# An LSTM with a mixture of experts behind it: when the router's small operations run, and which engine adds the residual

## The chip, the cores and the metric

One core of a Trainium2 chip runs the whole program. The metric is the device time of one execution in microseconds. The engines are PE (matrix products), DVE (VectorE), ACT (ScalarE), POOL (GpSimd) and SP, which starts transfers.

## The reference

Two sequences of 1,024 tokens with 256 features, all in float32. First an LSTM with 256 units over time, with a residual; then a layer of experts, with a residual again:

```python
def step(carry, xw_t):                     # 1024 times, one after the other
    prev_h, prev_c = carry
    a = xw_t + prev_h @ Wh                 # (2, 256) @ (256, 1024)
    i, f, o = sigmoid(a[:, :256]), sigmoid(a[:, 256:512]), sigmoid(a[:, 512:768])
    next_c = f * prev_c + i * tanh(a[:, 768:])
    next_h = o * tanh(next_c)
    return (next_h, next_c), next_h

x = x + lstm(x, h0=cond)                   # "x + h", called x2 in the kernel
shared = mean over 2 of  (silu(x @ w1.T) * (x @ w3.T)) @ w2.T     # hidden 512
s = sigmoid(concat(x, cond) @ W_router.T)  # 8 scores a token
# the two best of s + router_bias; gates = their s, divided by their sum
routed = sum over 8 of  gate[e] * (gelu(x @ r1[e].T) @ r2[e].T)   # hidden 256
out = x + (shared + routed) / 4
```

Only the LSTM is a chain: step t + 1 needs h of step t. The experts need x + h of their tokens and nothing else.

## The kernel before

**The recurrence.** A Python loop over `t` writes out 1,024 steps; `grp, u = divmod(t, 16)`. In each step PE multiplies h by the weights into two PSUM tiles (L541, 20 products, two records each in the profile), DVE transposes both (L568), ACT takes sigmoid and tanh (L571, L572), DVE and ACT make the new cell (L575, L579, L580, L588), and DVE the new h (L591, two halves). Each engine works through its instructions in the order in which the program issues them, so the order of issue decides what stands between two steps.

**Groups.** The tokens go through the experts in groups of steps, `GROUPS`: seven of 128 steps, then two of 64 (numbered 0 to 8; group 6 ends with step 895, group 7 with 959, group 8 with 1023). When a group's last step is done, `experts` puts its matrix products as units in a list `fill.pe`: 116 units for 128 steps, 90 for 64. They are worked off beside the steps of the following groups. `PACES` says in how many steps they should be done.

**The queues.** The class `Fill` holds a list for each engine. After the recurrent products of a step, `run_pe` issues up to two units (`ROOM`), or one where a projection of the inputs of the next 16 steps runs (u of 1, 6 or 11). Where fewer are issued, products with an identity matrix fill the place (L556). A unit that opens a PSUM bank is issued only if a bank is free; there are two (`fill.banks`), and `let_go` gives one back when DVE has read it. At the step's end, ACT's pieces are issued up to a cost of 1.0 (not where u is 8), and DVE's up to 0.5, first in first out; each piece carries a cost in the queue's own numbers and the first step in which it may run.

**DVE's pieces.** Of each shared product: multiply by the sigmoid (L340) and by the second product (L344); of each routed product: two multiplications (L364); then the sums: the start of a sum (L393) and one addition for each expert (L412, `add_expert`), which needs the gates of the router.

**The router.** PE makes the scores (L236), DVE adds the part of the condition (L254), ACT takes the sigmoid (L262), and `choose` lists 23 small DVE operations (L272 to L312) on 8 or 16 elements a partition, which end in the gates. `to_aside` puts them in the DVE queue with a cost of 0.18 each; only for the last group do they go to a list of their own, `aside`.

**x + h.** At the end of each 16th step (u of 15) `residual` adds x and the h of 16 steps on GpSimd into `x2T` (L485), and where a group ends it adds the one step left over. In the middle of the next 16 steps, DVE copies one element of it (`met`, L625), from u of 8 and t over 16 on.

**The end.** At step 1023 `drain` works off what is left of the groups before; then group 8 is put in, with six banks, and `drain` is called again: rounds of four units, ACT's pieces, DVE's pieces and three of `aside`. The outputs leave with a transfer for each 64 steps (L419).

Of the kernel before, what the change touches and what calls it, by code (L numbers as in the profile page):

```python
# [9 lines left out]
F32 = mybir.dt.float32  # L10
# [6 lines left out]
P = 128  # L17
# [6 lines left out]
TB = ROWS // N  # L24
# [11 lines left out]


ROOM = 2
WARM = 5
OUT_SCALE = 1.0 / (NS + TOP_K)  # L40
RSQRT2 = 0.7071067811865476
# [6 lines left out]
class Fill:  # L48
# [16 lines left out]
    def to_act(self, cost, fn, lag=0):  # L65
        self.add(self.act, cost, fn, lag)

    def to_dve(self, cost, fn, lag=1):
        self.add(self.dve, cost, fn, lag)

    def to_aside(self, cost, fn):
        if self.last:
            self.aside.append(fn)
        else:
            self.to_dve(cost, fn)

    def run_aside(self, count):
        for _ in range(min(count, len(self.aside))):
            self.aside.popleft()()

    def run(self, queue, budget):
        while queue and queue[0][0] <= self.step and queue[0][1] <= budget:
# [18 lines left out]
def lstm_moe_kernel(  # L101
# [16 lines left out]
    nc = tc.nc  # L118
# [57 lines left out]
    x2T = const.tile([P, K, T, N], F32, name="x2T")  # L176
# [4 lines left out]
    stepp = ctx.enter_context(tc.tile_pool(name="step", bufs=3))  # L181
# [4 lines left out]
    fill = Fill()  # L186

    def bank():
        if fill.last:
            pool, name = behind[0]  # L190
            behind.rotate(-1)
        else:
            pool, name = fill_ps, "ps_f"
        return pool.tile([P, 2, 256], F32, name=name)
# [10 lines left out]
    def condition_scores(lg, k):  # L205
        nc.tensor.matmul(
            lg, cond_b[:, k].rearrange("p s n -> p (s n)"), wr_sb[:, K + k, :],
            start=(k == 0), stop=(k == K - 1), skip_group_check=True,
        )
        if k == K - 1:  # L210
            fill.to_dve(0.25, lambda: keep_scores(lg))

    def keep_scores(lg):
        nc.vector.tensor_copy(cond_lg, lg)
        fill.let_go()

    def experts(t0, S):
# [10 lines left out]
        def toks(a, i):  # L228
            return a[:, i * P : (i + 1) * P]
# [13 lines left out]
        def big(name):  # L243
            return route.tile([P, NT, E], F32, name=name)
# [15 lines left out]
        def squash():  # L260
            st["s"] = big("s")
            nc.scalar.activation(st["s"], st["z"], AF.Sigmoid)  # L262
            for fn in choose():
                fill.to_aside(0.18, fn)

        def choose():

# [128 lines left out]
        def routed_down(i, e2, j):  # L396
            if j == 0:
                st["down"] = bank()
            ps, half, h = st["down"], j // (HR // P), j % (HR // P)
            c = (2 * e2 + half) * (HR // P) + h  # L400
            nc.tensor.matmul(  # L401
                ps[:, half, :], toks(st["h_r"][:, c, :], i), r2_sb[:, c, :],
                start=(h == 0), stop=(h == HR // P - 1), skip_group_check=True,
            )
            if j == 2 * (HR // P) - 1:
                for half in range(2):
                    fill.to_dve(0.5, lambda half=half: add_expert(i, 2 * e2 + half, ps[:, half, :]))

        def add_expert(i, e, ps):
            fill.run_aside(len(fill.aside))  # L410
            acc = st["acc", i]
            nc.vector.scalar_tensor_tensor(  # L412
                acc, ps, st["gate"][:, i, e : e + 1], acc, ALU.mult, ALU.add
            )
            if e % 2:
                fill.let_go()
            if e == E - 1:
                t = t0 + i * (P // N)
                nc.sync.dma_start(out=out_tn[t : t + P // N], in_=acc)  # L419
# [36 lines left out]
    def h_at(t):  # L456
        return hs[t // TB % 2][:, t % TB]

    def h_cols(t):
        u = t % TB  # L460
        return h_at(t)[:, :, N * u : N * (u + 1)]
# [16 lines left out]
    def gates_tile():  # L478

        tiles = [gates_ps.tile([P, 4, P], F32, name=f"ps{m}") for m in range(K)]  # L480
        return [a[:, 0] for a in tiles], [a[:, 1] for a in tiles], tiles[0][:, 2:]

    def residual(grp, u0, u1):
        t0 = grp * TB - 1
        nc.gpsimd.tensor_add(  # L485
            x2T[:, :, t0 + u0 : t0 + u1, :],
            xT_sb[:, :, t0 + u0 : t0 + u1, :],
            diags[grp % 2][:, u0:u1].rearrange("p u (k r) -> p k u r", r=ROWS)[:, :, :, :N],
        )

    ends, e0 = {}, 0
# [28 lines left out]
    nxt, nxt_turned, busy = gates_tile()  # L520
    for i in range(WARM):
        nc.tensor.matmul(
# [6 lines left out]
    for t in range(T):  # L529
        fill.step = t  # L530
        grp, u = divmod(t, TB)
        if u == 0:
            ps, turned = nxt, nxt_turned
            nxt, nxt_turned, busy = gates_tile()
            fresh = True
            sgm, gf = nxt_results


        for k, m, c0, c1 in BLOCKS:
            for q in range(Q):  # L540
                nc.tensor.matmul(  # L541
                    ps[m][q * ROWS : (q + 1) * ROWS][:, c0:c1],
                    h_at(t)[:, k, :],
                    wh_sb[:, k, q * D + m * P + c0 : q * D + m * P + c1],
                    start=False,
                    stop=(u == TB - 1 and k == K - 1),
                    skip_group_check=True,
                )
        ahead = t + TB < T and u in (1, 6, 11)
        if ahead:  # L550
            project(nxt, grp + 1, u // 5 - 1)
            fresh = False
        left = max(1, due - t)
        done = fill.run_pe(min(ROOM - ahead, -(-len(fill.pe) // left)))
        for _ in range(ROOM - done - ahead):
            nc.tensor.matmul(  # L556
                busy, ident, ident.unsqueeze(1).to_broadcast([P, 2, P]),
                start=fresh, stop=False, skip_group_check=True,
            )
            fresh = False  # L560
        rows = slice(N * u, N * (u + 1))

        gT = [turned[m].rearrange("p (a r) -> p a r", r=ROWS) for m in range(K)]
        c_new = [cells[m][:, t % 2] for m in range(K)]
        seen = [stepp.tile([P, N], F32, name=f"seen{m}") for m in range(K)]

        def transpose(m):
            nc.vector.transpose(turned[m], ps[m])  # L568

        def squash(m):  # L570
            nc.scalar.activation(sgm[:, u, m, :, :, 1], gT[m][:, 0:3, rows], AF.Sigmoid)  # L571
            nc.scalar.activation(gf[:, u, m, :, 0], gT[m][:, 3, rows], AF.Tanh)  # L572

        def forget(m):
            nc.vector.tensor_mul(gf[:, u, m, :, 1], sgm[:, u, m, 1, :, 1], c_prev[m][:, :, 1])  # L575

        def cell(m):

            nc.vector.tensor_copy(seen[m], gf[:, u, m, :, 0])  # L579
            nc.vector.tensor_tensor_scan(  # L580
                c_new[m].rearrange("p n z -> p (n z)"),
                sgm[:, u, m, 0].rearrange("p n z -> p (n z)"),
                gf[:, u, m].rearrange("p n z -> p (n z)"),
                0.0, ALU.mult, ALU.add,
            )

        def squash_cell(m):
            nc.scalar.activation(cells[m][:, 2, :, 0], c_new[m][:, :, 1], AF.Tanh)  # L588

        def output(m):  # L590
            nc.vector.tensor_mul(h_cols(t + 1)[:, m], sgm[:, u, m, 2, :, 1], cells[m][:, 2, :, 0])  # L591

        for fn in (transpose, squash):
            for m in range(K):
                fn(m)
        for m in range(K):
            forget(m)
            cell(m)
            squash_cell(m)
        for m in range(K):  # L600
            output(m)
        if u == TB // 2 and t + TB < T:
            nxt_results = results()
        else:
            fill.run(fill.act, 1.0)
        c_prev = c_new
        if u == TB - 1:
            residual(grp, int(grp == 0 or t - TB in ends), TB)
        if t == 2 * TB:
            lg = bank()[:, 0, :E]  # L610
            fill.banks -= 1
            fill.pe.extend((0, lambda k=k: condition_scores(lg, k)) for k in range(K))
        if t in ends:
            residual(grp + 1, 0, 1)
            if t == T - 1:
                drain(fill)
                fill.last = True
                fill.banks += 4
            t0, S, pace = ends[t]
            experts(t0, S)  # L620
            due = t + pace
        if u == TB // 2 and t > TB:

            met = stepp.tile([P, 1], F32, name="met")
            nc.vector.tensor_copy(met, x2T[:, 0, t - u - 2, :1])  # L625
        fill.run(fill.dve, 0.5)
    drain(fill)


def drain(fill):  # L630

    while fill.pe or fill.act or fill.dve:
        fill.step += 1
        fill.run_pe(4)
        fill.run(fill.act, 100.0)
        fill.run(fill.dve, 100.0)
        fill.run_aside(3)


# [63 lines left out]
```

## Time and profile before

| | |
|---|---|
| median of 3 runs | 2315.3 us (2314.7 to 2316.05) |
| profiled execution | 2314.89 us |
| its span, first to last instruction | 2313.1 us |
| granted clock of TensorE | 1.000 |
| busy: PE, DVE, ACT, POOL | 2220.1, 1701.6, 885.3, 25.9 us |
| L485 on POOL, 73 times | 328 ns median, 205 to 353 |
| L625 on DVE, 63 times | 9.2 us in all |

In a line of the profile's groups stand the line of the code, the engine, the operation, what is written from what is read, the shape of one instruction and the number of them; behind the bar the busy time in microseconds, the mean duration of one in nanoseconds, and the time that the engine stood idle just before them, with what ended it. A row of the timeline starts with the start and the duration in microseconds; PEld is the loading of weights, which may run ahead of the products. A row of the chain has start, duration and what was being done.

### The profile page before, as it was taken

How to read it: one execution, taken by the hardware profiler on the slowest of the kernel's cores; microseconds unless marked ns; L12 is line 12 of the kernel's file. 1: busy time of each engine (PE TensorE's matmuls, PEld its weight loads, DVE VectorE, ACT ScalarE, POOL GpSimd, SP SyncE). 2: the span in 40 equal slices, each digit the busy share in tenths (PEclk: the TensorE clock that was granted, in tenths of full speed). 3: DMA queues.
4: the chain of work that ended last, by engine and by line, in shares of the span. 5: the costliest groups of instructions: out<-in, count | busy, mean ns of one | idle time of the engine just before them, and what ended most of it. 6: DMA issues, size and time to landing. Idle time of an engine off the chain costs nothing.

```text
span 2313.1 us, 115407 instructions
## 1 busy us (share of the span) xinstructions
PE 2220.1 (96%) x48816; PEld 1574.3 (68%) x48816; DVE 1701.6 (74%) x10961; ACT 885.3 (38%) x6427; POOL 25.9 (1%) x82
## 2 busy tenths in 40 slices
PE   9999999999999999999999999999999999999978
PEld 6666666666666666666666666666666666666657
DVE  5666677777777777777777777777777777777775
ACT  3333334433334333443334333343333433344342
POOL 0000000000000000000000000000000000000000
PEclk9999999999999999999999999999999999999999
DMA  5000000000000000000000000000000000000000
GB/s 203 3 3 3 3 3 3 3 6 5 3 3 4 5 6 3 3 3 6 6 3 3 3 6 5 3 3 3 5 6 3 3 3 5 6 3 3 8 4 7
DMA packets 9705, 21.03 MB, mean 9 GB/s; under 512 B 1761, under 2 KB 7137, under 8 KB 8930
## 3 DMA queue, kind: packets, MB, share of 16 engines
q1 hardware_dynamic: 8898, 12.61, 1.6%
q8 instruction: 381, 6.24, 1.1%
q14 instruction: 138, 1.13, 0.2%
q10 hardware_dynamic: 288, 1.05, 0.1%
HBM read 11.56 MB, written 2.10 MB: 6 GB/s over the span
## 4 chain that ended last, share of the span: by engine, by line
DVE 59%; PE 37%; issue 3%; DMA 0%; SPq 0%; ACT 0%
PE ps L541 35%; DVE ps L568 29%; DVE c L580 12%; DVE results L575 8%; DVE seen L579 7%; DVE h L591 3%; PE ps L321 0%; PE ps_f L401 0%; PE ps_f L321 0%; PE ps L401 0%; DMA wh_sb<-in_wh_dram 0%; PE ps_f L383 0%; PE ps L383 0%; PE ps L556 0%; DVE acc L412 0%
## 5 line engine op out<-in xcount | busy, mean ns | idle before, releaser
L541 PE MATMUL ps<-wh_sb,h 128*32 128x128 f32 (+1 forms) x40960 | 1112.7, 254 | 86.9 <-DVE h L591 22.9
L541 PEld LDWEIGHTS ps<-wh_sb,h 128*32 128x32 f32 x40960 | 837.3, 109 | 489.9 <-DVE h L591 488.0
L568 DVE STREAM_TRANSPOSE ps<-ps 128x128 f32<-128x128 f32 x2048 | 677.8, 332 | 416.4 <-PE ps L541 415.0
L571 ACT ACTIVATE results<-ps 128x6 f32<-128x6 f32 x2048 | 362.9, 177 | 1167.3 <-DVE ps L568 1071.5
L556 PE MATMUL ps<-ident 128*128 128x256 f32 x1954 | 575.4, 391 | 0.0
L591 DVE TENSOR_TENSOR h<-results,c 128x2 f32<-128x2 f32 x2048 | 314.2, 153 | 168.2 <-ACT c L588 168.1
L556 PEld LDWEIGHTS ps<-ident 128*128 128x128 f32 x1954 | 351.4, 189 | 83.3 <-issue 45.1
L588 ACT ACTIVATE c<-c 128x2 f32<-128x2 f32 x2048 | 321.5, 157 | 220.1 <-DVE c L580 180.6
L580 DVE TENSOR_TENSOR_SCAN c<-results 128x4 f32<-128x4 f32 x2048 | 359.0, 175 | 0.0
L572 ACT ACTIVATE results<-ps 128x2 f32<-128x2 f32 x2048 | 340.4, 166 | 0.0
L579 DVE COPY seen<-results 128x2 f32<-128x2 f32 x2048 | 330.9, 162 | 0.0
L575 DVE TENSOR_TENSOR results<-results,c 128x2 f32<-128x2 f32 x2048 | 320.7, 157 | 0.0
L321 PE MATMUL ps_f<-x2T,r_sb 128*128 128x256 f32 (+1 forms) x800 | 166.8, 360 | 0.0
L321 PE MATMUL ps_f<-x2T,w_sb 128*128 128x256 f32 (+1 forms) x800 | 166.6, 360 | 0.0
L401 PE MATMUL ps_f<-r_sb,h_r 128*128 128x256 f32 x488 | 162.0, 424 | 0.0
L321 PEld LDWEIGHTS ps_f<-x2T,r_sb 128*128 128x128 f32 (+1 forms) x800 | 77.8, 153 | 42.7 <-issue 42.0
L321 PEld LDWEIGHTS ps_f<-x2T,w_sb 128*128 128x128 f32 (+1 forms) x800 | 77.6, 153 | 42.5 <-issue 41.8
L401 PEld LDWEIGHTS ps_f<-r_sb,h_r 128*128 128x128 f32 x488 | 75.4, 188 | 43.4 <-issue 40.5
L383 PE MATMUL ps_f<-w_sb,h_s 128*128 128x256 f32 x240 | 80.1, 425 | 0.0
L469 PE MATMUL ps<-wx_sb,xT_sb 128*32 128x128 f32 x2048 | 79.4, 273 | 0.0
L412 DVE SCALAR_TENSOR_TENSOR acc<-ps_f,gate,acc 128x256 f32<-128x256 f32 x122 | 58.2, 477 | 4.4 <-PE ps_f L401 4.2
L469 PEld LDWEIGHTS ps<-wx_sb,xT_sb 128*32 128x32 f32 x2048 | 58.6, 110 | 0.0
(81 smaller groups left out, 473.5 us busy)
## 6 DMA issues: line engine op xcount, KB each, us to landing
r_sb<-in_r_w1T_dram SPq DMA_DIRECT2D x1, 2048.0 KB, 17.2
r_sb<-in_r_w2T_dram SPq DMA_DIRECT2D x1, 2048.0 KB, 18.5
out_dram<-acc SPq DMA_DIRECT2D x16, 128.0 KB, 2.1
xT_sb<-in_xT_dram SPq DMA_DIRECT2D x6, 256.0 KB, 6.5
wx_sb<-in_wx_dram ACTq DMA_DIRECT2D x2, 512.0 KB, 4.2
wh_sb<-in_wh_dram SPq DMA_DIRECT2D x2, 512.0 KB, 4.4
w_sb<-in_s_w1T_dram SPq DMA_DIRECT2D x1, 1024.0 KB, 7.6
w_sb<-in_s_w3T_dram SPq DMA_DIRECT2D x1, 1024.0 KB, 9.6
```

The costliest lines, as they stand in the source:

```text
L321: nc.tensor.matmul(ps[r : r + rows, half, :W], w[:, k, c * P + r : c * P + r + rows], mov[k], start=(k == 0), stop=(k == K - 1), skip_grou ...
L401: nc.tensor.matmul(ps[:, half, :], toks(st["h_r"][:, c, :], i), r2_sb[:, c, :], start=(h == 0), stop=(h == HR // P - 1), skip_group_check= ...
L541: nc.tensor.matmul(ps[m][q * ROWS : (q + 1) * ROWS][:, c0:c1], h_at(t)[:, k, :], wh_sb[:, k, q * D + m * P + c0 : q * D + m * P + c1], sta ...
L556: nc.tensor.matmul(busy, ident, ident.unsqueeze(1).to_broadcast([P, 2, P]), start=fresh, stop=False, skip_group_check=True,)
L568: nc.vector.transpose(turned[m], ps[m])
L571: nc.scalar.activation(sgm[:, u, m, :, :, 1], gT[m][:, 0:3, rows], AF.Sigmoid)
L572: nc.scalar.activation(gf[:, u, m, :, 0], gT[m][:, 3, rows], AF.Tanh)
L575: nc.vector.tensor_mul(gf[:, u, m, :, 1], sgm[:, u, m, 1, :, 1], c_prev[m][:, :, 1])
L579: nc.vector.tensor_copy(seen[m], gf[:, u, m, :, 0])
L580: nc.vector.tensor_tensor_scan(c_new[m].rearrange("p n z -> p (n z)"), sgm[:, u, m, 0].rearrange("p n z -> p (n z)"), gf[:, u, m].rearrang ...
L588: nc.scalar.activation(cells[m][:, 2, :, 0], c_new[m][:, :, 1], AF.Tanh)
L591: nc.vector.tensor_mul(h_cols(t + 1)[:, m], sgm[:, u, m, 2, :, 1], cells[m][:, 2, :, 0])
```

## The change

The router's 23 operations always go to `aside`, and `run_dve` replaces the plain run of the DVE queue: it takes the head of the queue if that may run and fits into what is left of the budget, and otherwise one operation of `aside` for 0.18. An expert's addition is marked `late`: it doesn't run while `aside` holds anything. In steps with u of 15, DVE gets no piece; there it does `residual`, which moves from GpSimd to VectorE. The copy `met` goes. In `drain`, DVE's budget is 1.2 a round and covers both lists.

```diff
+ASIDE = 0.18
...
-    def to_dve(self, cost, fn, lag=1):
-        self.add(self.dve, cost, fn, lag)
-
-    def to_aside(self, cost, fn):
-        if self.last:
-            self.aside.append(fn)
-        else:
-            self.to_dve(cost, fn)
-
-    def run_aside(self, count):
-        for _ in range(min(count, len(self.aside))):
-            self.aside.popleft()()
+    def to_dve(self, cost, fn, lag=1, late=False):
+
+        self.dve.append((self.step + lag, cost, fn, late))
+
+    def run_dve(self, budget):
+        while True:
+            ready, cost, fn, late = self.dve[0] if self.dve else (0, 0.0, None, True)
+            if fn and ready <= self.step and cost <= budget and not (late and self.aside):
+                self.dve.popleft()
+            elif self.aside and budget >= ASIDE:
+                cost, fn = ASIDE, self.aside.popleft()
+            else:
+                return
+            budget -= cost
+            fn()
...
             nc.scalar.activation(st["s"], st["z"], AF.Sigmoid)
-            for fn in choose():
-                fill.to_aside(0.18, fn)
+            fill.aside.extend(choose())
...
-                    fill.to_dve(0.5, lambda half=half: add_expert(i, 2 * e2 + half, ps[:, half, :]))
+                    fill.to_dve(0.5, lambda half=half: add_expert(i, 2 * e2 + half, ps[:, half, :]), late=True)
 
         def add_expert(i, e, ps):
-            fill.run_aside(len(fill.aside))
...
     def residual(grp, u0, u1):
         t0 = grp * TB - 1
-        nc.gpsimd.tensor_add(
+        nc.vector.tensor_add(
...
         c_prev = c_new
-        if u == TB - 1:
-            residual(grp, int(grp == 0 or t - TB in ends), TB)
         if t == 2 * TB:
...
+        if u < TB - 1:
+            fill.run_dve(0.5)
+            continue
+        residual(grp, int(grp == 0 or t - TB in ends), TB)
         if t in ends:
             residual(grp + 1, 0, 1)
...
-        if u == TB // 2 and t > TB:
-
-            met = stepp.tile([P, 1], F32, name="met")
-            nc.vector.tensor_copy(met, x2T[:, 0, t - u - 2, :1])
-        fill.run(fill.dve, 0.5)
     drain(fill)
 
 
 def drain(fill):
 
-    while fill.pe or fill.act or fill.dve:
+    while fill.pe or fill.act or fill.dve or fill.aside:
         fill.step += 1
         fill.run_pe(4)
         fill.run(fill.act, 100.0)
-        fill.run(fill.dve, 100.0)
-        fill.run_aside(3)
+        fill.run_dve(1.2)
```

## The prediction

> **What bounds the kernel now.** I read the page first: busy shares, then the chain that ended last.
>
> ```profile
> PE 2220.1 (96%) x48816; PEld 1574.3 (68%) x48816; DVE 1701.6 (74%) x10961; ACT 885.3 (38%) x6427; POOL 25.9 (1%) x82
> ...
> DVE 59%; PE 37%; issue 3%; DMA 0%; SPq 0%; ACT 0%
> ...
> L568 DVE STREAM_TRANSPOSE ps<-ps 128x128 f32<-128x128 f32 x2048 | 677.8, 332 | 416.4 <-PE ps L541 415.0
> ...
> L556 PE MATMUL ps<-ident 128*128 128x256 f32 x1954 | 575.4, 391 | 0.0
> ```
>
> PE's 96% is padded: 1954 records (977 matmuls) of L556 only fill time. The chain is the LSTM recurrence: L541, transposes, cell, output, next step. DVE waits 415.0 us for L541, so there is a gap of about 0.4 us a step in which DVE's pieces run unseen. Taking the first L568 of each step from the timeline, 1,002 of 1,023 step intervals are 2.21 us, with no piece (512 steps) as with the costliest, L412 at 0.477 us together with L625 at 0.146 us (12 steps). The rest: three early steps (8, 11 and 15), and 18 steps of 2.29 us, all with u = 15. The timeline at one of these (step 447):
>
> ```profile
> 999.22 0.70 PE L321 MATMUL ps_f<-x2T,r_sb 128*128 128x256 f32 x2
> ...
> 1000.00 0.35 POOL L485 TENSOR_TENSOR x2T<-xT_sb,h 128x64 f32<-128x64 f32 x1 [35.06 <-DVE c L580]
> ...
> 1000.12 0.26 DVE L580 TENSOR_TENSOR_SCAN c<-results 128x4 f32<-128x4 f32 x1
> ...
> 1001.32 0.66 DVE L568 STREAM_TRANSPOSE ps<-ps 128x128 f32<-128x128 f32 x2 [0.23 <-PE ps L541]
> ```
>
> GpSimd's x + h starts when a matmul that reads x2T has ended (999.92) and runs beside the scan, which takes 0.26 us where 0.175 is usual (L580's mean). Eighteen scans are long, in these 18 steps.
>
> Then the end, from the chain in order of time and the timeline:
>
> ```profile
> 2271.04 1.09 PE ps L541 x40
> 2272.12 3.65 PE ps_f L383 x16
> 2275.77 6.91 PE ps_f L401 x32
> 2282.68 0.34 PE ps L236 x4
> ```
>
> ```profile
> 2273.35 0.16 DVE L591 TENSOR_TENSOR h<-results,c 128x2 f32<-128x2 f32 x1 [0.17 <-ACT c L588]
> 2273.43 0.47 DVE L364 SCALAR_TENSOR_TENSOR h_r<-er,ps_f 128x128 f32<-128x128 f32 x2
> 2273.59 0.20 POOL L485 TENSOR_TENSOR x2T<-xT_sb,h 128x4 f32<-128x4 f32 x1 [1.88 <-DVE h L591]
> ...
> 2282.30 0.63 PEld L236 LDWEIGHTS ps<-wr_sb,x2T 128*128 128x128 f32 x4
> ```
>
> The last x2T is ready at 2273.79, but the last group's scores start loading at 2282.30: PE first works through 48 records (two per matmul, so 24 units) of the group before. That backlog is on the path.
>
> **Part 1: the router's 23 operations step aside.** Following the queue rules of the old code step by step (two banks, 0.5 of DVE per step, 1.0 of ACT, two units of PE, one where a projection runs) gives 977 fillers and 24 units queued before PE takes its share of step 1023: exactly the 1954 records and the 48 above, and the number of pieces in every step as in the timeline. So the rules can be trusted for the new code.
>
> Old: 23 operations, two a step, fill 12 steps of the DVE queue, first in first out. The first two shared products hold both banks behind them, and PE takes no unit for a stretch: eight steps or more in each group of 128, and steps 983 to 991 in group 7 (counting from 0; 64 long). At step 960 the queue holds 27 + 90 = 117 units. Steps 960 to 1023 run 95, so 22 are left over after step 1023 took two.
>
> New: pieces go first, the 23 operations fill steps without one (steps 974 to 997 in group 7). No such stretch is left. At step 960 the queue holds 19 + 90 = 109 units, 8 fewer, and the steps run all 109, 14 more: 8 + 14 = 22. PE's last unit of group 7 falls in step 1021; one addition is left for the drain. The late rule (an expert's addition waits while the router has operations) never costs: group 6's last operation comes in step 944, its first addition in step 947; group 7's in 997 and 1016. Units run earlier only replace L556 fillers, and no step gets more than the 0.5 budget, so the 2.21 us holds.
>
> **Part 2: x + h on VectorE.** Removed: 63 copies L625 at 146 ns, 73 GpSimd adds. Added on DVE: 64 adds of 60 or 64 elements and 9 of 4 elements. The 64-element form is not in the trace on DVE. Below it lie L272 (128x16, 167 ns) and above it L344 (128x128, 290 ns), though that one reads PSUM; on the line between them, 167 + 48 x 123 / 112 = 220 ns, which I take; the 4-element one is about 155 ns (L591 takes 153). It sits behind the output of u = 15, where the new code runs no piece, so DVE's load there is 0.22 us, or 0.37 where a group ends, against L412 plus L625 (0.62) that cost nothing. Cost: nothing, covered by L541; uncovered it would be 64 x 0.22 = 14.1 us.
>
> The wait moves with it. GpSimd waited for PE's x2T reader of the same step; now DVE does, at 29 of the 64 adds by the new order. Behind it on DVE's queue stand the next transposes. In step 447 that reader ended at 999.92, DVE comes to the add after L591 of 1000.61, and PE itself went on with L541 at 1000.50: the wait is over by then, since PE cannot start the next step before its units. With two units it ends about 0.43 us later (L321's 428 ns), 1000.35, still before. Nothing else on the queues of SP or GpSimd is passed.
>
> The long scans go: 18 x 0.083 = 1.5 us, all on the chain. The page "SBUF — State Buffer" of the Trainium skill (section "Who interferes with whom") says that a VectorE instruction with two SBUF inputs and a GpSimd one that reads SBUF lock each other out for the whole instruction. Were that full, the scan could only begin at 1000.35, end at 1000.52 and cost 0.14 us more; then 18 steps would give 4.0 us. The scan ended at 1000.38 and the step grew by 0.083, so the trace agrees on who collides and not on how much, and 1.5 stands.
>
> **Part 3: the end.** After step 1023 PE has two fillers, then waits for x + h. DVE's first add follows L591 at 2273.43 (L364's place) to 2273.65; the 4-element add needs the last L591 (ends 2273.51) and overlaps the first, about 2273.57 to 2273.72; PE follows DVE by 0.05 us elsewhere (L591 at 2270.83 + 0.15, L541 at 2271.03): scores load at 2273.77 instead of 2282.30, 8.5 us earlier. Behind that nothing differs: the order of the last group's 90 units, pieces and router operations (three per round, as before) comes out the same under the budget of 1.2, and PE bounds it from 2282.68 until 2309.10. What is late next is PE's own work. Bounds: issue gaps of up to 0.9 us lie in this stretch (0.63 us at 2295.26), and may go or come: 7.6 to 9.4.
>
> **Sum.** 1.5 + 8.5 = 10.0 us. The profiled execution took 2314.89 us (span 2313.1), so 2304.9; the median of the runs, 2315.3, lies 0.4 above it: 2305.3 us. A measurement can tell about 0.2% (4.6 us) from no change.
>
> **Rivals.**
> - *The scans stay long for another reason.* Only the backlog goes: 2315.3 - 8.5 = 2306.8. For it: little; against: 18 long scans, each with POOL busy beside it. 5%.
> - *The backlog stays.* PE's stretches without units have another cause than the router (a bank held by something else), so the change doesn't do what it says: 2315.3 - 1.5 = 2313.8. Against: the rules reproduce every step. 4%.
> - *x + h lies open on DVE.* Its wait or its length outlasts L541: 64 x 0.22 = 14.1 us of new chain, 2315.3 - 10.0 + 14.1 = 2319.4, slower. It decides once more than 10.0 / 64 = 0.16 us of each add is uncovered. For it: DVE holds 59% of the chain, and its wait is new there. Against: 12 steps with 0.62 us of pieces at 2.21. 4%.
> - *PE's clock falls in the lull before the last group.* L522 at the start took 650 ns, L556 391: at that rate the 26.4 us of PE work from 2282.68 to 2309.10 grow by 66%, 17.5 us: 2322.8, slower. Against: the lull is about 0.6 us (two fillers end near 2273.18, by the 1.13 us that two take elsewhere), and PE idles 0.69 us before L541 in steps at 2262 with no loss. 1%. The page "TensorE: Matmul & The Clock Gate" (Part 1) puts the drop after an idle window of about 3.4 us; by that rule this rival does not occur, and the row of 0.69 us agrees as far as it goes.
>
> **Numbers.** Forecast 86%. Its own range is 10.0 with 0.9 either way and the scatter of the runs shown (0.6 below, 0.75 above the median): 2303.8 to 2307.0. Reaching to the first rival and its scatter gives 2303.7 to 2307.5; left out are the others, 9%, and some edge. Faster 0.91 (forecast and first rival), same 0.04, slower 0.05.
>
> **What would show it.** L556 falls from 1954 records to 1910 (22 fillers fewer); no L383 or L401 of `ps_f` between the last L541 and the last group's L236; L485 on DVE with a mean near 0.2 us; no L580 over 0.2 us; steps at u = 15 at 2.21. I would be wrong if steps at u = 15 grew, if PE's first L236 of the last group came later than 1 us after the last L591, or if the stretch behind it were longer than 30.8 us (2313.1 - 2282.30).

## The result, and the profile after

The changed kernel takes 2304.82 us in the median of 6 runs (2304.3 to 2305.64), beside 2314.83 us (2314.62 to 2316.05) for the kernel before: ratio 0.9956, 95% interval 0.9943 to 0.9969, 10.0 us less. The profiled execution took 2304.3 us with a span of 2302.5 us, 10.6 us less than the span before; it is the fastest of the six, and 10.6 is what the following adds up to.

In the new file the numbers shift: the recurrent products are L543, the transposes L570, the scan L582, the output L593, x + h L487, the fillers L558, the scores L240, the expert sums L414. From the page:

```profile
PE 2210.7 (96%) x48772; PEld 1566.5 (68%) x48772; DVE 1706.1 (74%) x10971; ACT 886.2 (38%) x6427; POOL 2.6 (0%) x9
...
DVE 60%; PE 37%; issue 3%; DMA 0%; SPq 0%; ACT 0%
...
L558 PE MATMUL ps<-ident 128*128 128x256 f32 x1910 | 562.9, 391 | 0.0
```

The busy shares hardly move, and the chain has nearly the same split: neither says that the kernel is faster. The line that does is the last, 1910 records where there were 1954.

The timeline at step 447, the step that was shown of before:

```profile
998.43 0.70 PE L324 MATMUL ps_f<-x2T,r_sb 128*128 128x256 f32 x2
...
999.33 0.17 DVE L582 TENSOR_TENSOR_SCAN c<-results 128x4 f32<-128x4 f32 x1
...
999.73 0.16 DVE L593 TENSOR_TENSOR h<-results,c 128x2 f32<-128x2 f32 x1 [0.16 <-ACT c L590]
999.80 0.22 DVE L487 TENSOR_TENSOR x2T<-xT_sb,h 128x64 f32<-128x64 f32 x1
1000.44 0.66 DVE L570 STREAM_TRANSPOSE ps<-ps 128x128 f32<-128x128 f32 x2 [0.42 <-PE ps L543]
```

The scan is back at 0.17 us. x + h takes DVE 0.22 us behind L593, after the reader of x2T has ended (999.13), and DVE still waits 0.42 us for PE before the transposes. No scan of this run is longer than 0.2 us; of the step intervals, 1,020 of 1,023 are 2.21 us, and the three others are the early steps 8, 11 and 15.

The end, from the chain in order of time:

```profile
2271.73 0.16 DVE h L593
2271.88 0.22 DVE x2T L487 x2
2272.10 0.14 issue
2272.24 0.58 PE ps L240 x4
```

Between the last output and the last group's scores there is x + h and nothing else. By the chain the scores begin 0.51 us after the last L593 begins, where they began 9.33 us after it (2282.68 - 2273.35): 8.8 us. The loop up to that L593 is 1.6 us shorter (2273.35 and 2271.73), and the stretch from the scores to the end 0.15 us (30.43 and 30.28). 8.8 + 1.6 + 0.15 = 10.6.

### The profile page after: what moved, and what is told of

Same layout as the page of the kernel before. It is cut to its first block, busy times and chain, and to the rows that moved or that the text cites. A ratio compares the mean times of both kernels' runs of the same rounds, so it can differ in the third digit from the quotient of the medians.

```text
span 2302.5 us, 115226 instructions
## 1 busy us (share of the span) xinstructions
PE 2210.7 (96%) x48772; PEld 1566.5 (68%) x48772; DVE 1706.1 (74%) x10971; ACT 886.2 (38%) x6427; POOL 2.6 (0%) x9
## 4 chain that ended last, share of the span: by engine, by line
DVE 60%; PE 37%; issue 3%; DMA 0%; SPq 0%; ACT 0%
PE ps L543 36%; DVE ps L570 29%; DVE c L582 12%; DVE results L577 8%; DVE seen L581 7%; DVE h L593 3%; PE ps L324 0%; PE ps_f L324 0%; PE ps L404 0%; DMA wh_sb<-in_wh_dram 0%; PE ps L386 0%; PE ps_f L404 0%; PE ps L558 0%; DVE acc L414 0%; DVE b_sb L133 0%
## 5 line engine op out<-in xcount | busy, mean ns | idle before, releaser
L543 PE MATMUL ps<-wh_sb,h 128*32 128x128 f32 (+1 forms) x40960 | 1112.7, 254 | 85.7 <-DVE h L593 23.2
L543 PEld LDWEIGHTS ps<-wh_sb,h 128*32 128x32 f32 x40960 | 837.3, 109 | 487.6 <-DVE h L593 485.8
L570 DVE STREAM_TRANSPOSE ps<-ps 128x128 f32<-128x128 f32 x2048 | 677.1, 332 | 406.5 <-PE ps L543 406.2
L558 PE MATMUL ps<-ident 128*128 128x256 f32 x1910 | 562.9, 391 | 0.0
L593 DVE TENSOR_TENSOR h<-results,c 128x2 f32<-128x2 f32 x2048 | 315.2, 154 | 167.7 <-ACT c L590 167.6
L558 PEld LDWEIGHTS ps<-ident 128*128 128x128 f32 x1910 | 344.6, 189 | 80.3 <-issue 42.3
L582 DVE TENSOR_TENSOR_SCAN c<-results 128x4 f32<-128x4 f32 x2048 | 358.4, 175 | 0.0
L414 DVE SCALAR_TENSOR_TENSOR acc<-ps_f,gate,acc 128x256 f32<-128x256 f32 x122 | 58.3, 478 | 0.8 <-PE ps_f L404 0.7
```

Of the source, the lines that this page charges most:

```text
L543: nc.tensor.matmul(ps[m][q * ROWS : (q + 1) * ROWS][:, c0:c1], h_at(t)[:, k, :], wh_sb[:, k, q * D + m * P + c0 : q * D + m * P + c1], sta ...
L558: nc.tensor.matmul(busy, ident, ident.unsqueeze(1).to_broadcast([P, 2, P]), start=fresh, stop=False, skip_group_check=True,)
L582: nc.vector.tensor_tensor_scan(c_new[m].rearrange("p n z -> p (n z)"), sgm[:, u, m, 0].rearrange("p n z -> p (n z)"), gf[:, u, m].rearrang ...
```

## The experiments

My theory: the router's place in DVE's queue stopped PE's units, and the units left over at the end cost PE's time; x + h on GpSimd cost the 18 long scans and, once on VectorE, costs nothing. The rivals were those of the prediction: that the gain belongs to x + h, that the stops have another cause, that x + h lies open on VectorE, that the scans were long for another reason. Beside the first four kernels, the kernel before took 2314.4 us; beside the others, 2314.54 us. The new kernel was not run again beside them, so a difference from its 2304.82 us can be off by the 0.4 us by which the kernel before varies.

**One part alone: the queue.** x + h stays on GpSimd, with its copy:

```diff
-        nc.vector.tensor_add(
+        nc.gpsimd.tensor_add(
...
+        if u == TB // 2 and t > TB:
+            met = stepp.tile([P, 1], F32, name="met")
+            nc.vector.tensor_copy(met, x2T[:, 0, t - u - 2, :1])
         if u < TB - 1:
             fill.run_dve(0.5)
```

> The new queue with x + h left on GpSimd (and its copy met). Theory (the backlog is the router's doing, 8.5 us or a little more; the long scans are GpSimd's, 0.083 us each): no units of group 7 are left over at step 1023, 1910 records of the filler; but units run earlier, so 24 steps at u = 15 instead of 18 have one reader of x2T and a long scan: 2304.8 + 24 x 0.083 + 0.1 = 2306.9 us. Rival, the gain belongs to x + h on VectorE: about 2314.8, the backlog there or its time spent elsewhere.

Measured: 2306.46 us, ratio 0.9965 (0.9952 to 0.9977). The fillers are at 1910 records, nothing of group 7 is left, and exactly 24 scans are long. The timeline of step 447:

```profile
1001.78 0.35 POOL L487 TENSOR_TENSOR x2T<-xT_sb,h 128x64 f32<-128x64 f32 x1 [35.07 <-DVE c L582]
1001.90 0.26 DVE L582 TENSOR_TENSOR_SCAN c<-results 128x4 f32<-128x4 f32 x1
```

Two things follow. The queue alone brings 7.9 of the 10.0 us; and by moving units forward it makes six more steps in which GpSimd's add meets a scan, 6 x 0.083 = 0.5 us, so the two parts are worth a little more together than one by one (the part that follows brings 1.2; the 0.4 us that are then missing are within the scatter). In the tail GpSimd was no slower: the scores begin 0.50 us after the last L593 begins (2275.84 and 2275.34).

**The other part alone: x + h.** The old queue, x + h on VectorE, no `met`:

```diff
-        nc.gpsimd.tensor_add(
+        nc.vector.tensor_add(
...
-        if u == TB // 2 and t > TB:
-
-            met = stepp.tile([P, 1], F32, name="met")
-            nc.vector.tensor_copy(met, x2T[:, 0, t - u - 2, :1])
```

> The old queue, x + h on VectorE, no met; steps at u = 15 run a piece beside the add. Theory: the long scans go, 18 x 0.083 = 1.5 us, the 24 units before the last group stay: 2314.8 - 1.5 = 2313.3 us, and no step over 2.21 us behind step 15. Rival, x + h lies open on VectorE: up to 64 x 0.22 = 14 us more, 2327; half-way, pieces of 0.48 us and the add together overrun the gap in some steps at u = 15.

Measured: 2313.2 us, ratio 0.9993 (0.9984 to 1.0002), so by the times alone not to be told from the kernel before. The profile settles it: no scan over 0.2 us, 1,018 steps at 2.21, the loop from the first transposes to the last 1.3 us shorter (2260.7 and 2262.0). The half-way rival shows in one step of u = 15, where the add meets two pieces: 2.228 us, of which the step behind gives back 0.02. The chain at the end has the backlog unchanged:

```profile
2270.73 3.65 PE ps_f L383 x16
2274.38 6.91 PE ps_f L401 x32
2281.28 0.34 PE ps L236 x4
```

**The order turned round.** Everything of the change stays, but the router's operations go first:

```diff
-            if fn and ready <= self.step and cost <= budget and not (late and self.aside):
+            if self.aside and budget >= ASIDE and not self.last:
+                cost, fn = ASIDE, self.aside.popleft()
+            elif fn and ready <= self.step and cost <= budget and not (late and self.aside):
```

> The new kernel with the order in run_dve turned round: the router's operations go ahead of the pieces (not in the last drain). x + h stays on VectorE. Theory: the PE stops come back; by the queue rules 32 units are left over after step 1023, 7 of them of the up products at about 0.22 us and 25 at 0.44, and 987 fillers are issued (1974 records). The lull and the fillers that they replace are worth 1.7 us, two units of step 1023 cost 0.4: 2304.8 + 12.6 + 0.4 - 1.7 = 2316 us, slower than the kernel before. Rival, the stops come from something other than the router's place: 2304.8.

Measured: 2317.52 us, ratio 1.0013 (1.0004 to 1.0022): slower than the kernel before, 12.7 us more than the new one, by the order of one queue. The fillers are at 1974 records, as counted. The chain:

```profile
2271.29 0.16 DVE h L595
2271.45 0.21 DVE x2T L489 x2
2271.66 0.43 DVE h_r L369 x2
2272.08 0.14 issue
2272.22 1.24 PE ps_f L326 x32
2273.46 0.64 PE ps_f L382 x4
2274.10 3.46 PE ps_f L388 x16
2277.55 6.91 PE ps_f L406 x32
2284.46 0.34 PE ps L242 x4
```

The scores begin 13.2 us after the last L595, 12.7 us later than in the new kernel, 1.4 more than I had expected. Most of that is one wait that my sum left out: the first of the remaining units had to wait for a bank which two pieces, L369, give back behind x + h (0.43 us in the chain), and the timeline has PE idle for 1.07 us before 2272.22, where I had counted the lull as filled. The profiled span is only 11.4 us longer (2313.9 and 2302.5), with a stretch behind the scores that is 0.8 us shorter (29.48), while 2.9 us and not 1.8 lie outside the span; why, stays open. The rival, stops with another cause, falls.

**Units left over without the router.** In the new kernel, group 7 is paced more slowly:

```diff
-PACES = [128] * 6 + [84, 60, 0]
+PACES = [128] * 6 + [84, 75, 0]
```

> The new kernel with the pace of group 7 set from 60 steps to 75, so that its units are issued more slowly and 10 are left over after step 1023 by the queue rules (965 fillers, 1930 records), with no change to the router. Theory (a unit left over costs PE's time, 0.44 us): 12 units from step 1023 on, less the 1.7 us of fillers and lull that they replace: 2304.8 + 5.3 - 1.7 = 2308.4 us. Rival, what is left over at the end is hidden or the gain has another source: 2304.8.

Measured: 2308.06 us, ratio 0.9971 (0.9959 to 0.9982), 3.2 us more than the new kernel where 3.6 were expected; 1930 filler records. The chain:

```profile
2271.69 0.16 DVE h L593
...
2272.06 0.41 DVE acc L414
...
2272.51 3.72 PE ps_f L404 x16
2276.23 0.34 PE ps L240 x4
```

So it is the units at the end that cost, whoever left them there.

**More work behind x + h.** Two or six adds of the same size on VectorE, with results that nothing uses:

```diff
+    pads = [const.tile([P, K, TB, N], F32, name=f"pad{i}") for i in range(2)]
...
         residual(grp, int(grp == 0 or t - TB in ends), TB)
+        for pad in pads if t < T - 1 else []:
+            now = xT_sb[:, :, t - u : t - u + TB, :]
+            nc.vector.tensor_add(pad, now, now)
```

> The new kernel with two more VectorE adds of 64 elements behind each x + h (63 steps at u = 15; results unused). Theory: DVE has about 0.64 us between the last L593 and the next transposes plus 0.08 of overlap, and adds follow one another every 0.14 us: 0.14 x 2 + 0.22 = 0.50 us fits, nothing is lost: 2304.8 us. Rival, x + h lies open on VectorE and so does anything behind it: 2 x 0.14 x 63 = 18 us more, 2322.

Measured: 2304.74 us, ratio 0.9955 (0.9942 to 0.9969). Step 447 in the timeline:

```profile
998.96 0.22 DVE L488 TENSOR_TENSOR x2T<-xT_sb,h 128x64 f32<-128x64 f32 x1
999.10 0.35 DVE L620 TENSOR_TENSOR pad<-xT_sb 128x64 f32<-128x64 f32 x2
999.60 0.66 DVE L571 STREAM_TRANSPOSE ps<-ps 128x128 f32<-128x128 f32 x2 [0.15 <-PE ps L544]
```

With three times the work, DVE still waits 0.15 us for PE.

> The same with six more adds. Theory: 0.14 x 6 + 0.22 = 1.06 us, 0.34 over the gap of 0.72, in 63 steps: 21 us more, 2326. Rival, open: 6 x 0.14 x 63 = 53 us more, 2358. If DVE's slack is larger than read, less than 10 us more.

Measured: 2322.94 us, ratio 1.0036 (1.0022 to 1.0049), 18.1 us more than the new kernel. All 63 steps with the adds are longer, 2.53 us in the mean, that is by 0.32 us, of which the step behind gives 0.02 back. Step 447:

```profile
1009.62 0.89 DVE L620 TENSOR_TENSOR pad<-xT_sb 128x64 f32<-128x64 f32 x6
1010.43 0.52 DVE L571 STREAM_TRANSPOSE ps<-ps 128x128 f32<-128x128 f32 x2
```

The transposes start only when the adds are nearly done (1010.51), 1.02 us after the last L594 began (1009.41) where it was 0.71 us with two adds. Together the two show where the cover ends: the rival that x + h lies open is out, and it decides from a load of about 0.7 us on, not from 0.22.

**GpSimd beside the scan, on purpose.** Two adds on GpSimd, with results that nothing uses, each in a quarter of the steps:

```diff
+    clash = [const.tile([P, 32, N], F32, name=f"clash{i}") for i in range(2)]
...
+        if u in (3, 7, 11, 15):
+            nc.gpsimd.tensor_add(
+                clash[0], xT_sb[:, 0, :32, :],
+                sgm[:, u, 0, 0, :, 1].unsqueeze(1).to_broadcast([P, 32, N]),
+            )
         for m in range(K):
             forget(m)
...
+        if u in (1, 5, 9, 13):
+            nc.gpsimd.tensor_add(
+                clash[1], xT_sb[:, 0, :32, :],
+                h_cols(t + 1)[:, 0].unsqueeze(1).to_broadcast([P, 32, N]),
+            )
         if u < TB - 1:
```

> The new kernel with two kinds of GpSimd adds of 64 elements put in (results unused): at u of 3, 7, 11, 15 one that waits for the first half's sigmoids, so that it runs beside the scan, and at u of 1, 5, 9, 13 one that waits for the first half of the new h, so that it runs beside L543 and DVE's pieces. Theory: each scan that meets the add takes 0.26 us in place of 0.175, its step 2.29, so 256 steps give 21 us, 2326; the others stay at 2.21. By a full lock of the instruction, a scan waits for the add's end and costs 0.2 us a step, 2356. Rival, the long scans of before had another cause: all steps stay at 2.21, 2305.

Measured: 2322.91 us, ratio 1.0035 (1.002 to 1.0049). The timeline of one of the steps in which the add waits for the sigmoids:

```profile
455.26 0.29 POOL L600 TENSOR_TENSOR clash<-xT_sb,results 128x64 f32<-128x64 f32 x1 [3.33 <-ACT results L575]
...
455.34 0.24 DVE L583 TENSOR_TENSOR_SCAN c<-results 128x4 f32<-128x4 f32 x1
```

254 scans are long, 0.242 us in the median; the steps with u of 3, 7, 11 and 15 take 2.266 us, those with u of 1, 5, 9 and 13 stay at 2.208. So the cause of the long scans is settled, and GpSimd's add beside L544 and the pieces is free. The step grows by 0.058 and not by 0.083, in part because here the add starts 0.08 us ahead of the scan and lasts 0.29, where it started 0.12 ahead and lasted 0.35: the scan is 0.067 us longer and not 0.083. It is also the first of the step's two scans and not the second; what that does was not tried. A further 0.06 us is lost in each step with u = 0, in 62 steps, which I had not expected (below): 252 x 0.058 + 62 x 0.06 = 18.3 us, and 18.1 were measured.

The second kind of add shows which of VectorE's instructions are held:

```profile
326.92 0.29 POOL L620 TENSOR_TENSOR clash<-xT_sb,h 128x64 f32<-128x64 f32 x1 [4.97 <-DVE h L594]
326.94 0.16 DVE L594 TENSOR_TENSOR h<-results,c 128x2 f32<-128x2 f32 x1 [0.16 <-ACT c L591]
327.01 0.23 DVE L305 TENSOR_TENSOR hot<-hot,hot 128x16 f32<-128x16 f32 x1
```

L594, whose input c lies in PSUM, takes its 0.16 us inside the add. L305, an operation of the router with both inputs in SBUF, takes 0.23 us where 0.167 is usual (L301 in the kernel before), and ends 0.03 us behind the add, as the scans do. Router operations with one SBUF input (L287, 0.161 us) and the pieces that read PSUM (L415, 0.478 us) are not held.

**Pieces in steps of u = 15.** The edit puts them ahead of x + h, not behind it as the expectation has it; the load is the same:

```diff
+        if t < T - 1:
+            fill.run_dve(0.5)
         residual(grp, int(grp == 0 or t - TB in ends), TB)
```

> The new kernel with DVE's pieces run in steps of u = 15 too, behind x + h. By the queue rules none of group 7 is left over either way. Theory: 0.14 + 0.48 = 0.62 us fits into 0.72, so 2304.8 us, and leaving the place free was not needed. Rival, the add and a piece of 0.41 to 0.48 overrun the gap at u = 15: 0.05 to 0.1 us in some 37 steps, 2 to 4 us, 2307 to 2309.

Measured: 2304.23 us, ratio 0.9954 (0.994 to 0.9968), against 2304.82 with the place left free: no difference beyond the scatter. Steps at u = 15 are 2.208 us in the median; the two longest behind step 15, 2.227 and 2.219 us, are those in which two pieces and the add come together.

Step 447 in the timeline:

```profile
1000.32 0.41 DVE L367 SCALAR_TENSOR_TENSOR h_r<-er,ps_f 128x256 f32<-128x256 f32 x1
1000.65 0.22 DVE L487 TENSOR_TENSOR x2T<-xT_sb,h 128x64 f32<-128x64 f32 x1
1000.96 0.66 DVE L570 STREAM_TRANSPOSE ps<-ps 128x128 f32<-128x128 f32 x2
```

The bracket behind the transposes is gone: of DVE's idle time 0.09 us is left (from 1000.87 to 1000.96), and the step is no longer for it. That part of the change is caution, not gain. No version tried was measurably faster than the new kernel.

## Why the prediction was right, point by point

- *The router's place.* The count from the queue rules came true to the record: 1954, 1910, 1974 and 1930 fillers in four orders. Reversed, the order made the kernel slower; the stops are the router's. One reading is off without weight: the trace of before has no unit in steps 982 to 992, where I wrote 983 to 991; the counts of units hold all the same.
- *The wait of an expert's addition for the router* was held to cost nothing, and nothing of it shows: no unit is left and the addition that is left for the drain runs beside the scores. That rule by itself was not tried, nor was the removal of `met` by itself.
- *The long scans.* 18 x 0.083 = 1.5 us was the term; the loop between the first and the last transposes is 1.52 us shorter (2262.04 and 2260.52).
- *x + h on VectorE.* 220 ns was the price from the two rows around it, 219 ns the measured mean (155 for the small form, as said). It lies in the gap, which has room for three of them. The moved wait is nowhere late.
- *The end.* 8.5 us was the term. The scores' weights start loading 0.48 us after the last L593 begins where 0.42 was expected, since PE followed DVE by 0.11 us and not 0.05. By the chain the move is worth 8.8, as PE takes the first product right behind the load when nothing runs before it: 0.03 us here, 0.38 in the chain before. That excess is within the 0.9 of the bound. GpSimd in its place would have been as quick there (0.50 against 0.51 us by the chain).
- *The step that failed*, without weight in the sum, is what I worked out from the Trainium skill's page "SBUF — State Buffer" (section "Who interferes with whom"). I read its full lock as "the scan's whole time again after GpSimd's add", got 0.23 us a step and held the row of 0.083 against it. In all 18 long scans of before, all 24 of the queue alone and all 254 of the forced case, the scan ends 0.027 to 0.032 us behind the end of the add. So the lock is full; what is left to do after it is 0.03 us, not 0.175, and how much a scan loses depends on how much of the add is still to come. The same slip stands in the expectation of 2356 us for the forced case. The full lock is what that page of the Trainium skill states, and the instructions that the forced case shows held are those that it names, with two SBUF inputs.
- *The rivals.* Scans long for another reason: out. Backlog unchanged: out. x + h open: out up to three times its work. The clock: granted 1.000, and PE idled 0.68 us before the scores with 30.28 us behind, no more than before. The longest lull at the end of any run is the 1.07 us of the order turned round, also at a granted clock of 1.00; a longer one was not tried.
- *The sum.* That the medians differ by 10.0 us, as forecast to the digit, is partly luck: the terms of the two profiles add up to 10.6 us, and the runs of one kernel scatter by over 1 us.

## What to carry to other kernels

When small, dependent operations share a first-in-first-out queue with pieces that give back scarce buffers, count which step each falls in: here 23 operations of under 0.2 us cost nothing where they ran, and 22 units of PE's work at the far end of the program. A busy engine that partly runs fillers says nothing about room; the number of fillers does, and a replay of the queue rules gives it before anything is run. Work moves for nothing onto the engine of the critical chain if it falls into a gap that the chain itself leaves, and adding copies of it until the step grows measures that gap.

## What the runs showed of the hardware beyond that

Where a VectorE instruction of the chain has to wait for two engines, the second wait cost 0.06 us, though it had long been fulfilled. In the forced case, the first L578 of each 16 steps writes to a tile that GpSimd has read two groups of 16 steps before, and the trace has one more semaphore instruction there:

```profile
L578 DVEq EVENT_SEMAPHORE  x62: 21/21/21, 83.3 to 2256.7; - x62
```

By the trace this instruction waits for ACT's sigmoids, and L578 behind it for GpSimd; L578 starts 0.10 us after the sigmoids' end (83.344 and 83.242) where it is 0.03 us in the next step (85.544 and 85.511). These steps, u = 0, take 2.268 us in the median, with no long scan in them. The early step 15, 2.265 to 2.270 us in the kernels without additions of mine there, is alike: in the kernel before it has the only such instruction of L591. That `met` is there to take such waits out of the chain would fit, but was not tried.
